# Two mixture-of-experts stages: the last experts' answers as rows, paired half-block experts, additions placed ahead, and a stored result split by tiles

## The chip, the cores and the metric

The kernel is one launch on 1 core of a Trainium2 chip. The time is the device time of that core in microseconds (us). Before the change the median of three runs is 1690.21 us (1686.34 to 1697.15).

## The reference, cut to what matters

A two-layer perceiver works on x (512 tokens of 512 numbers, float32) with a context of 8192 tokens. Each layer adds cross attention, self attention and a mixture-of-experts feed-forward stage (FFN) to x. The change lies in the two FFN stages and in the store of the final x.

```python
x = x + _L0_xattn_ref(_layernorm(x), ctx_1024, ...)
x = x + _L0_attn_ref(_layernorm(x), ...)
x = x + _L0_ffn_ref(_layernorm(x), router, W1, W2)     # 8 experts, 512 -> 2048 -> 512, silu
x = x + _L1_xattn_ref(_layernorm(x), ctx_1024, ...)
x = x + _L1_attn_ref(_layernorm(x), ...)
x = x + _L1_ffn_ref(_layernorm(x), Wg, W1, W2)         # 8 experts, 512 -> 1024 -> 512, relu squared
...
    top_v, top_i = jax.lax.top_k(logits, 2)            # each token goes to 2 of the 8 experts
    ...
    for e in range(E):
        h = act(xf @ W1[e])
        out = out + gates[:, e:e + 1] * (h @ W2[e])
```

## The kernel before, in words

**Experts by rank.** In `ffn` the router's two choices for each token are counted, and the experts are ordered by how many tokens they have (`by_rank`, L1584). The expert of rank r has room for `caps[r]` tokens (`CAPS0` for the first layer, `CAPS1` for the second, L38 and L39); all rooms lie one after another along one axis, rank r beginning at `starts[r]`. A flag says whether some expert has more tokens than room; then `rest` (L1942) works off what is left under `tc.If(flag > 0)` (L1937). In the runs here the flag is 0, and every engine jumps over that block.

**Pieces.** An expert's hidden width is cut into n pieces of 512 (n = 4 in the first layer, 2 in the second). Each piece needs 1 MB of W1 and 1 MB of W2, loaded by `weights` (L1715) from SyncE's queue (SP) into four buffers each; piece i+4's load waits until piece i's matmuls have left the buffer. `hidden(i)` (L1816) computes the hidden layer of piece i transposed: 16 matmuls (L1826) with a 128x128 block of W1 as the stationary operand and the expert's k tokens as the columns that stream; ScalarE and VectorE apply the activation (`silu` L2020, `relu_squared` L2025). `back(i)` (L1833) does the same with W2 (L1842) and gathers an expert's answer in one PSUM tile `y`, transposed; after the last piece ScalarE and VectorE copy it to `answers` (L1851, L1853). The loop at L1884 runs hidden(i) and then back(i-1), so that TensorE has a piece to work on while the activation of the next is made. A float32 matmul is two records in the profile (two passes), a transpose one.

**Tokens in, answers out.** Tokens of rank 0 are gathered by matmul (`gather`), the others by indirect DMA in blocks of 128 rows (`transposed`, L1798), each transposed on TensorE (L1811) and copied by ScalarE (L1812). Answers go the opposite way in blocks of 128 rows: `store` (L1863) transposes a block with `rows_of` (TensorE L1858, ScalarE L1860 into one of two `yb` buffers) and GpSimd's queue (POOL) writes it to DRAM (L1867). When all are stored, eight indirect DMAs on POOL fetch for each tile of 128 tokens its first and second answer (`got`, L1912), and eight VectorE operations add them, times their gates, to x (L1920).

**The last experts.** The experts from `by_dma` on don't pass through DRAM: 112 rows of room in both layers (one expert of 112 in the first, two of 64 and 48 in the second; `split` is where they begin, `tail` their size). Their answers are turned into rows (`yb`, L1921) and multiplied by a gated one-hot matrix `gb` (L1917) in the final matmul (L1925). Another matmul adds x itself through the identity (L1924). In the first layer `x_from` (L216) takes statistics of the sum (L219, VectorE) and copies it to x (L220, ScalarE); in the second layer the sums are only copied to x (L1931).

**Order.** Each engine executes its list of instructions in order. The order across pieces comes from a scheduler that sees this code, so a wait keeps back whatever stands behind it on its engine. After the flag's block the final x is stored by one 1 MB DMA (`store_x`, L2056, issued by SP); then all engines load one more number (L2071) and jump over a second block (L2075) that a larger count would need.

Of the kernel before, what the change touches and what calls it, by code (L numbers as in the profile page):

```python
# [10 lines left out]
F32 = mybir.dt.float32  # L11
# [5 lines left out]
ALU = mybir.AluOpType  # L17
# [3 lines left out]
P = 128  # L21
# [16 lines left out]
CAPS0 = (132, 160, 152, 148, 140, 124, 116, 112)  # L38
CAPS1 = (112, 256, 224, 192, 160, 96, 64, 48)  # L39
BAND = 64  # L40
# [17 lines left out]
def tile_perceiver(  # L58
# [1649 lines left out]
    def ffn(wp, pool, w1, w2, ff, layer, act, softmax_first, caps, order):  # L1708
# [20 lines left out]
        with ExitStack() as st:  # L1729
# [23 lines left out]
            def get(i):  # L1753
                if i not in pieces and i < E * n:
                    pieces[i] = weights(experts[i // n], i % n)
                return pieces.get(i)

# [5 lines left out]
            accs = {}  # L1763

            by_dma = E - 1
            while total - starts[by_dma - 1] <= P:
                by_dma -= 1
            split = starts[by_dma]
            tail = total - split

            def one_hot(to, r, gated):
# [26 lines left out]
            def transposed(b):  # L1798
# [15 lines left out]
                return go  # L1814

            def hidden(i):  # L1816
                r, c = divmod(i, n)
                k = caps[r]
# [13 lines left out]

            def back(i, hT):  # L1833
                r, c = divmod(i, n)
                k = caps[r]
# [19 lines left out]
            def rows_of(src, lo, m, name, bufs=2):  # L1855
                ps = psum.tile([P, S], F32, name="stp", tag="m")
                for c in range(NC):
                    nc.tensor.transpose(ps[0:m, c * P : (c + 1) * P], src[:, c, lo : lo + m], ident)  # L1858
                to = inner.tile([P, S], F32, name=name, tag=name, bufs=bufs)
                nc.scalar.copy(to[0:m, :], ps[0:m, :])  # L1860
                return to
# [21 lines left out]
            last, done, blk = None, 0, 0  # L1883
            for i in range(E * n):  # L1884
                hT = hidden(i)
                for j in range(1, 4):
                    get(i + j)
                if last is not None:
# [8 lines left out]
                if i % n == n - 2 and r + 1 < E:  # L1897
                    while waiting and waiting[0][0] * P < starts[r + 1] + caps[r + 1]:
                        waiting.pop(0)[1]()
                        fetch()  # L1900
# [4 lines left out]
                if i == n * by_dma + 1:  # L1905
# [11 lines left out]
                    gb = rows_of(gated, 0, tail, "gb", 1)  # L1917
            back(E * n - 1, last)
            for got, g, t in late:
                nc.vector.scalar_tensor_tensor(x[:, t, :], got, g, x[:, t, :], ALU.mult, ALU.add)  # L1920
            yb = rows_of(answers, split, tail, "yb")  # L1921
            for t in range(NT):
                ps = psum.tile([P, D], F32, name="xps", tag="h", bufs=4)
                nc.tensor.matmul(ps, lhsT=ident, rhs=x[:, t, :], start=True, stop=False)  # L1924
                nc.tensor.matmul(  # L1925
                    ps, lhsT=gb[0:tail, t * P : (t + 1) * P], rhs=yb[0:tail, :], start=False, stop=True
                )
                if layer == 0:
                    x_from(t, ps)
                else:  # L1930
                    (nc.scalar.copy if t % 2 else nc.vector.tensor_copy)(x[:, t, :], ps)  # L1931

# [4 lines left out]
        with tc.If(flag > 0):  # L1937
            rest(wp, pool, weights, irow, place, gate, xn, n, act, caps)
            for t, st in stats.items():
                nc.vector.bn_stats(st, x[:, t, :])  # L1940
# [114 lines left out]

    def store_x():  # L2056
        nc.sync.dma_start(out=out.rearrange("b (t p) d -> p (b t) d", p=P), in_=x)

# [10 lines left out]
    rest_of_layer1()  # L2069
    store_x()  # L2070
    n = nc.values_load(  # L2071
# [3 lines left out]
    with tc.If(n > SLOTS):  # L2075
# [16 lines left out]
        rest_of_layer1()  # L2092
        store_x()

# [108 lines left out]
```

## Time and profile before

| | us |
|---|---|
| median of three runs | 1690.21 (1686.34 to 1697.15) |
| the profiled execution | 1685.11 |
| its span, first to last instruction | 1683.3 |
| busy in the span: TensorE (PE) / its weight loads (PEld) | 1551.2 / 925.3 |
| busy: VectorE (DVE) / ScalarE (ACT) / GpSimd (POOL) | 767.9 / 601.5 / 449.7 |
| mean granted TensorE clock | 0.946 of full |
| last piece's matmuls of the second layer end | 1658.74 |
| last copy of the sum into x ends | 1672.61 |
| the store of x is issued, and its time to landing | 1673.61, 5.5 |

The profiled execution lies 1.8 us above its span and 5.1 us below the median. In timeline rows the columns are start, duration, engine, line, operation and tiles, count, and in brackets the idle time of that engine before it and what ended the idle time. Rows whose engine ends in q are of an engine's sequencer. "Chain" rows give start, duration and what the end of the program depended on.

### The profile page before, as it was taken

How to read it: one execution, taken by the hardware profiler on the slowest of the kernel's cores; microseconds unless marked ns; L12 is line 12 of the kernel's file. 1: busy time of each engine (PE TensorE's matmuls, PEld its weight loads, DVE VectorE, ACT ScalarE, POOL GpSimd, SP SyncE). 2: the span in 40 equal slices, each digit the busy share in tenths (PEclk: the TensorE clock that was granted, in tenths of full speed). 3: DMA queues.
4: the chain of work that ended last, by engine and by line, in shares of the span. 5: the costliest groups of instructions: out<-in, count | busy, mean ns of one | idle time of the engine just before them, and what ended most of it. 6: DMA issues, size and time to landing. Idle time of an engine off the chain costs nothing. (4 is left out here: it accounts for less than half of the span.)

```text
span 1683.3 us, 25532 instructions
## 1 busy us (share of the span) xinstructions
PE 1551.2 (92%) x10565; PEld 925.3 (55%) x10565; DVE 767.9 (46%) x1373; ACT 601.5 (36%) x1132; POOL 449.7 (27%) x345
## 2 busy tenths in 40 slices
PE   5899899999999986999999899999999999879996
PEld 2344333333244446999998456433433245469995
DVE  5366677775525553111112133667775518631101
ACT  2366365556632241111111311165557522301110
POOL 6000077777110011000002100078786110010001
PEclk9999899999999897999999999989999999779996
DMA  7155100000120005877785400000000220075562
GB/s 251 48 183 164 50 1 1 1 2 1 46 86 1 1 2 217 318 255 266 272 307 165 132 26 19 26 1 1 1 1 1 106 57 2 26 277 205 194 227 85
DMA packets 83936, 169.42 MB, mean 101 GB/s; under 512 B 5107, under 2 KB 20499, under 8 KB 82385
## 3 DMA queue, kind: packets, MB, share of 16 engines
q1 hardware_dynamic: 77200, 147.87, 26.0%
q0 software_dynamic: 6016, 17.55, 3.0%
q10 hardware_dynamic: 576, 2.10, 0.4%
q8 instruction: 89, 1.46, 0.4%
q14 instruction: 55, 0.44, 0.1%
HBM read 156.82 MB, written 9.63 MB: 99 GB/s over the span
## 5 line engine op out<-in xcount | busy, mean ns | idle before, releaser
L911 ACT ACTIVATE pT<-sc,kbias 128x512 f32<-128x512 f32 x480 | 298.3, 694 | 184.7 <-PE sc L667 142.6
L786 PE MATMUL sc<-qTf,kTf 32*128 32x512 f32 x1264 | 299.2, 657 | 2.0 <-DVE mx L799 1.1
L799 DVE SCALAR_TENSOR_TENSOR mx<-scm,kbias,mx 128x512 f32<-128x512 f32 x312 | 219.3, 745 | 72.4 <-PE scm L786 69.9
L786 PE MATMUL scm<-qTf,kTf 32*128 32x512 f32 x656 | 224.4, 670 | 10.2 <-DVE mx L799 10.2
L1842 PE MATMUL y<-hT,w 128*128 128x112 f32 (+13 forms) x1536 | 212.0, 298 | 1.1 <-DVE hT L2023 1.1
L1842 PEld LDWEIGHTS y<-hT,w 128*128 128x128 f32 x1536 | 205.4, 198 | 2.9 <-DVE hT L2023 1.2
L1826 PE MATMUL hps<-tokens,w 128*128 128x112 f32 (+13 forms) x1536 | 205.9, 293 | 0.0
L1826 PEld LDWEIGHTS hps<-tokens,w 128*128 128x128 f32 x1536 | 198.9, 192 | 1.7
L882 POOL TENSOR_TENSOR four<-four,pT 128x2048 f32<-128x2048 f32 x42 | 190.7, 4540 | 9.5 <-ACT pT L911 6.8
L786 PEld LDWEIGHTS sc<-qTf,kTf 32*128 32x128 f32 x1264 | 83.8, 187 | 121.0 <-issue 78.1
L861 PE MATMUL acc<-pT,vNf 128*32 128x256 f32 (+1 forms) x1600 | 146.5, 438 | 1.6 <-ACT o L871 1.6
L882 POOL TENSOR_TENSOR four<-pT 128x2048 f32<-128x2048 f32 x24 | 109.0, 4542 | 93.5 <-ACT pT L911 93.5
L799 DVE SCALAR_TENSOR_TENSOR mx<-sc,kbias,mx 128x512 f32<-128x512 f32 x136 | 93.2, 744 | 66.4 <-PE sc L786 66.4
L2023 DVE TENSOR_TENSOR hT<-sg,hps 128x264 f32<-128x264 f32 (+7 forms) x64 | 27.9, 437 | 191.1 <-ACT sg L2022 191.1
L861 PEld LDWEIGHTS acc<-pT,vNf 128*32 128x32 f32 x1600 | 32.1, 108 | 133.5 <-issue 127.7
L667 PE MATMUL sc<-shift,ones 3*128 3x512 bf16 (+3 forms) x544 | 95.0, 377 | 3.6 <-DVE shift L702 3.6
L1867 POOL DMA_DIRECT2D answers_d<-yb x17 | 9.4, 557 | 311.6 <-ACT yb L1860 311.6
L786 PEld LDWEIGHTS scm<-qTf,kTf 32*128 32x128 f32 x656 | 75.4, 190 | 17.8 <-DVE mx L799 17.8
L2022 ACT ACTIVATE sg<-hps 128x264 f32<-128x264 f32 (+7 forms) x64 | 25.4, 397 | 134.7 <-PE hps L1826 134.7
L2028 DVE TENSOR_TENSOR hT<-sg 128x224 f32<-128x224 f32 (+7 forms) x32 | 14.7, 459 | 107.7 <-ACT sg L2027 107.7
L1053 PE MATMUL pv<-wkvf,cslot 128*128 128x512 f32 x120 | 59.8, 641 | 3.4 <-ACT vNf L1062 3.3
L681 DVE TENSOR_REDUCE neg<-mtp 128x4 f32<-128x512 f32 x64 | 41.2, 684 | 40.2 <-PE mtp L678 40.2
(354 smaller groups left out, 1893.8 us busy)
## 6 DMA issues: line engine op xcount, KB each, us to landing
w<-in_L_ffn_W SPq DMA_DIRECT2D x96, 1024.0 KB, 7.6
mi<-in_mask SPq DMA_DIRECT2D x32, 512.0 KB, 4.3
cslot<-in_ctxT SPq DMA_DIRECT2D x30, 256.0 KB, 5.2
answers_d<-yb POOLq DMA_DIRECT2D x15, 256.0 KB, 7.1
answers_d<-zero POOLq DMA_DIRECT2D x9, 256.0 KB, 7.8
wkvf<-in_L_xattn_WkvT ACTq DMA_DIRECT2D x4, 512.0 KB, 6.6
wq<-in_L_xattn_WqT SPq DMA_DIRECT2D x2, 1024.0 KB, 8.5
wof<-in_L_xattn_WoT SPq DMA_DIRECT2D x2, 1024.0 KB, 4.7
```

The lines of the kernel that those rows point to most:

```text
L667: nc.tensor.matmul(ps, lhsT=ones16[r, :], rhs=k.shifts[g][r, 0:w], start=start, stop=stop)
L681: nc.vector.tensor_reduce(neg[:, h, :], tp.rearrange("p (t k) -> p t k", k=P), AX.X, ALU.max, negate=True)
L786: nc.tensor.matmul(ps, lhsT=kT[HD * h : HD * (h + 1), g, i * P : (i + 1) * P], rhs=qT[HD * h : HD * (h + 1), g, :], start=True, stop=stop,)
L799: nc.vector.scalar_tensor_tensor(to, ps, b, to, ALU.add, ALU.max)
L861: nc.tensor.matmul(k.sums[g][HD * h : HD * (h + 1), r], lhsT=vN[:, i, g * P + HD * h : g * P + HD * (h + 1)], rhs=pT[:, h, r], start=(i == ...
L882: engine.tensor_tensor(to, parts[g][-1], pT, ALU.add)
L911: nc.scalar.activation(pT[:, h, :], ps, AF.Exp, bias=kbias[:, i : i + 1])
L1053: last = nc.tensor.matmul(ps.rearrange("p (g n) -> p g n", g=NG), lhsT=src[:, c, s % 2, :], rhs=wkv[:, :, c, i * P : (i + 1) * P], start=( ...
L1826: nc.tensor.matmul(ps[:, j, 0:k], lhsT=w1[:, c, f * P : (f + 1) * P], rhs=tokens[:, c, starts[r] : starts[r] + k], start=(c == 0), stop=(c ...
L1842: nc.tensor.matmul(accs[0][:, d, 0:k], lhsT=w2[:, f, d * P : (d + 1) * P], rhs=hT[:, f, 0:k], start=(c == 0 and f == 0 and d % 2 == 0), st ...
L2022: nc.scalar.activation(sg, ps, AF.Sigmoid)
L2023: nc.vector.tensor_tensor(dst, sg, ps, ALU.mult)
```

## The change

The room of the last expert of the second layer grows from 48 to 64, so its last two experts fill half a block of 128 rows each; the sum of rooms becomes 1168 and takes a tenth block of 16 rows in the gather. These two experts are then worked side by side, in two units in place of four: unit c holds piece c of both. `hidden_rows` uses the tokens (128x64) as the stationary operand and streams W1 (512 columns); the first expert writes PSUM partitions 0 to 63, the second 64 to 127, matmul by matmul in turn. The activation runs once over 128x512, `transposed_rows` turns the result for the second product, and `back_rows` again streams W2 past 64 stationary columns for each expert, so that `y` holds rows. In the first layer the last expert (112 tokens) keeps `hidden` and only uses `back_rows`, with one expert. No answers of the last experts are copied to `answers` or transposed. The eight additions of `got` to x stand ahead of the last `back` in the code. In the second layer the matmul through the identity is gone; VectorE adds the product to x, and each tile of x is stored by its own 256 KB DMA, in front of the flag's block (and again inside it).

```diff
--- before.py
+++ after.py
@@ -36,7 +36,7 @@
 
 RANKS = (4, 0, 1, 2, 3, 5, 6, 7)
 CAPS0 = (132, 160, 152, 148, 140, 124, 116, 112)
-CAPS1 = (112, 256, 224, 192, 160, 96, 64, 48)
+CAPS1 = (112, 256, 224, 192, 160, 96, 64, 64)
 BAND = 64
 PAD = BAND // 2
 NW = S // BAND
@@ -1751,9 +1751,9 @@
             pieces = {}
 
             def get(i):
-                if i not in pieces and i < E * n:
+                if i not in pieces:
                     pieces[i] = weights(experts[i // n], i % n)
-                return pieces.get(i)
+                return pieces[i]
 
             for i in range(3):
                 get(i)
@@ -1761,12 +1761,19 @@
             tokens = inner.tile([P, NC, total], F32, name="tokens", tag="tokens", bufs=1)
             answers = inner.tile([P, NC, total], F32, name="answers", tag="answers", bufs=1)
             accs = {}
+
 
             by_dma = E - 1
             while total - starts[by_dma - 1] <= P:
                 by_dma -= 1
             split = starts[by_dma]
             tail = total - split
+            pair = E - by_dma == 2
+            assert pair and caps[by_dma:] == (P // 2,) * 2 or by_dma == E - 1
+            units = n * (by_dma + 1)
+            order_of = [[i] for i in range(n * by_dma)]
+            order_of += [[(r * n) + c for r in range(by_dma, E)] for c in range(n)]
+            inline = [i for u in order_of for i in u]
 
             def one_hot(to, r, gated):
                 for t in range(NT):
@@ -1813,7 +1820,55 @@
 
                 return go
 
+            def hidden_rows(i):
+
+                ws = [get(j)[0] for j in order_of[i]]
+                ps = psum.tile([P, S], F32, name="hrow", tag="h", bufs=4)
+                for c in range(NC):
+                    for j, w in enumerate(ws):
+                        lo = split + j * P // 2
+                        nc.tensor.matmul(
+                            ps[j * P // 2 : (j + 1) * P // 2, :], lhsT=tokens[:, c, lo : lo + P // 2], rhs=w[:, c, :],
+                            start=(c == 0), stop=(c == NC - 1),
+                        )
+                rows = inner.tile([P, S], F32, name="hN", tag="hN", bufs=2)
+                act(inner, rows, ps)
+
+                def transposed_rows():
+                    tp = psum.tile([P, NC, P], F32, name="htp", tag="m")
+                    for f in range(NC):
+                        nc.tensor.transpose(tp[:, f, :], rows[:, f * P : (f + 1) * P], ident)
+                    hT = inner.tile([P, NC, W], F32, name="hT", tag="hT", bufs=2)
+                    nc.scalar.copy(hT[:, :, 0:P], tp)
+                    return hT
+
+                return transposed_rows
+
+            def back_rows(i, hT):
+
+                c = i - n * by_dma
+                if pair:
+                    hT = hT()
+                if c == 0:
+                    accs[0] = pacc.tile([P, NC, W], F32, name="y", tag="y")
+                y = accs[0].rearrange("p d k -> p (d k)")[:, 0:D]
+                ws = [get(j)[1] for j in order_of[i]]
+                m = tail // len(ws)
+                for f in range(NC):
+                    for j, w in enumerate(ws):
+                        nc.tensor.matmul(
+                            y[j * m : (j + 1) * m, :], lhsT=hT[:, f, j * m : (j + 1) * m], rhs=w[:, f, :],
+                            start=(c == 0 and f == 0), stop=(c == n - 1 and f == NC - 1),
+                        )
+                if c < n - 1:
+                    return None
+                to = inner.tile([P, S], F32, name="yb", tag="yb", bufs=2)
+                nc.scalar.copy(to[0:tail, :], y[0:tail, :])
+                return to
+
             def hidden(i):
+                if pair and i >= n * by_dma:
+                    return hidden_rows(i)
                 r, c = divmod(i, n)
                 k = caps[r]
                 w1, _ = get(i)
@@ -1831,6 +1886,8 @@
                 return hT
 
             def back(i, hT):
+                if i >= n * by_dma:
+                    return back_rows(i, hT)
                 r, c = divmod(i, n)
                 k = caps[r]
                 _, w2 = get(i)
@@ -1881,10 +1938,10 @@
             for _ in range(3):
                 fetch()
             last, done, blk = None, 0, 0
-            for i in range(E * n):
+            for i in range(units):
                 hT = hidden(i)
-                for j in range(1, 4):
-                    get(i + j)
+                for j in inline[: inline.index(order_of[i][0]) + 4]:
+                    get(j)
                 if last is not None:
                     back(i - 1, last)
                     if i % n == 0:
@@ -1895,7 +1952,8 @@
                 last = hT
                 r = i // n
                 if i % n == n - 2 and r + 1 < E:
-                    while waiting and waiting[0][0] * P < starts[r + 1] + caps[r + 1]:
+                    end = total if r + 1 == by_dma else starts[r + 1] + caps[r + 1]
+                    while waiting and waiting[0][0] * P < end:
                         waiting.pop(0)[1]()
                         fetch()
                 if i == 1:
@@ -1915,20 +1973,21 @@
                             )
                             late.append((got, gates[:, j, t : t + 1], t))
                     gb = rows_of(gated, 0, tail, "gb", 1)
-            back(E * n - 1, last)
             for got, g, t in late:
                 nc.vector.scalar_tensor_tensor(x[:, t, :], got, g, x[:, t, :], ALU.mult, ALU.add)
-            yb = rows_of(answers, split, tail, "yb")
+            yb = back(units - 1, last)
             for t in range(NT):
                 ps = psum.tile([P, D], F32, name="xps", tag="h", bufs=4)
-                nc.tensor.matmul(ps, lhsT=ident, rhs=x[:, t, :], start=True, stop=False)
+                if layer == 0:
+                    nc.tensor.matmul(ps, lhsT=ident, rhs=x[:, t, :], start=True, stop=False)
                 nc.tensor.matmul(
-                    ps, lhsT=gb[0:tail, t * P : (t + 1) * P], rhs=yb[0:tail, :], start=False, stop=True
+                    ps, lhsT=gb[0:tail, t * P : (t + 1) * P], rhs=yb[0:tail, :], start=(layer > 0), stop=True
                 )
                 if layer == 0:
                     x_from(t, ps)
                 else:
-                    (nc.scalar.copy if t % 2 else nc.vector.tensor_copy)(x[:, t, :], ps)
+                    nc.vector.tensor_tensor(x[:, t, :], x[:, t, :], ps, ALU.add)
+                    store_x(t)
 
 
         flag = nc.values_load(
@@ -1936,6 +1995,9 @@
         )
         with tc.If(flag > 0):
             rest(wp, pool, weights, irow, place, gate, xn, n, act, caps)
+            if layer > 0:
+                for t in range(NT):
+                    store_x(t)
             for t, st in stats.items():
                 nc.vector.bn_stats(st, x[:, t, :])
 
@@ -2053,8 +2115,8 @@
         for t in range(NT):
             nc.sync.dma_start(out=x[:, t, :], in_=a["x"][0, t * P : (t + 1) * P, :])
 
-    def store_x():
-        nc.sync.dma_start(out=out.rearrange("b (t p) d -> p (b t) d", p=P), in_=x)
+    def store_x(t):
+        nc.sync.dma_start(out=out[0, t * P : (t + 1) * P, :], in_=x[:, t, :])
 
     c8 = const.tile([P, NKT], U8, name="c8")
     nc.sync.dma_start(out=c8, in_=a["key_mask"])
@@ -2067,7 +2129,6 @@
     nc.vector.tensor_tensor(worst, irow0[:, SLOTS : SLOTS + 1], irow1[:, SLOTS : SLOTS + 1], ALU.max)
     cross_slots1(irow1, kbias1)
     rest_of_layer1()
-    store_x()
     n = nc.values_load(
         worst, min_val=0, max_val=2 * NKT,
         skip_runtime_bounds_check_because="a count of at most NKT, or that and NKT",
@@ -2090,7 +2151,6 @@
                 osb.append(o)
             cross_attention1()
         rest_of_layer1()
-        store_x()
 
 
 # ---- launch: one core; the host lays the inputs out ----
```

## The prediction, made blind

> **What bounds the kernel now.** I read the page first, for busy shares and clock.
>
> ```profile
> PE 1551.2 (92%) x10565; PEld 925.3 (55%) x10565; DVE 767.9 (46%) x1373; ACT 601.5 (36%) x1132; POOL 449.7 (27%) x345
> PE   5899899999999986999999899999999999879996
> PEclk9999899999999897999999999989999999779996
> ```
>
> TensorE bounds nearly every slice. The change touches only the ends of the two FFN stages: about 895 to 935 us, and 1618 us to the end. So next come the chain of waits in order of time at the end, and busy time and clock of two stretches (the column before the last two is the clock).
>
> ```profile
> 1642.30 3.56 PE hps L1826 x32
> 1645.86 12.89 PE y L1842 x64
> ...
> 1659.05 0.04 DVE answers L1853
> ...
> 1662.67 2.08 PE xps L1924 x2
> ...
> 1672.02 0.59 ACT x L1931
> ```
>
> ```profile
> 1642.00:1644.00 2.00, 2.00 (x20) 2.00 (x20) 0.29 (x1) 0.35 (x2) 0.00 (x0) 1.00 0.00 0
> 1648.00:1650.00 2.00, 2.00 (x11) 2.00 (x11) 0.00 (x0) 0.00 (x0) 1.70 (x2) 0.50 0.27 49
> ```
>
> The last expert (48 tokens) takes 12.89 us for 64 records because the clock is halved; then VectorE's additions begin, and TensorE waits for them until 1662.67. Beside this runs another chain, seen in the timeline of POOL, VectorE and SP:
>
> ```profile
> 1645.11 0.54 POOL L1867 DMA_DIRECT2D answers_d<-yb  x1 [4.65 <-ACT yb L1860]
> 1647.75 1.02 POOL L1912 DMA_INDIRECT got<-answers_d,rows_of  x1 [2.11 <-DMA answers_d<-yb]
> 1656.61 0.94 POOL L1912 DMA_INDIRECT got<-answers_d,rows_of  x1 [0.30 <-DMA got<-answers_d,rows_of]
> 1659.22 5.38 DVE L1920 SCALAR_TENSOR_TENSOR x<-got,gates,x 128x512 f32<-128x512 f32 x8
> 1673.61 0.40 SPq L2057 DMA_DIRECT2D out_x<-x  x1
> ```
>
> The gathers start 2.64 us after the last store is issued, are issued over 8.9 us and land 3.7 us later (1660.3). Without TensorE's slow stretch they are what is late next.
>
> **The second layer, step by step, in the times of before.** The built order of the changed kernel gives the sequence.
>
> *Pair units.* A 512-column record costs 0.43 us here (two records of L1925 in 0.86). A pair layer is 8 matmuls, 16 records: 6.9 us one after another, 3.43 us if the two halves of 64 columns run at once. No 64-column pair is in the trace; the nearest row has four groups of 32 columns:
>
> ```profile
> 1164.81 3.48 PE den L891 x32
> ```
>
> 32 records of 512 columns in 3.48 us, where 13.8 would be one after another: 3.9 of 4. The Trainium skill speaks against full overlap: "TensorE: Matmul & The Clock Gate", Part 3, has 2.38 for three column tiles, 0.79 of ideal; two would then give 1.6, 4.3 us a layer, and three such layers ahead of the stores would cost 2.6 us more. I take the row, 3.43; the bounds are 3.43 and 6.9.
>
> *To the last store.* Before, hidden(12) began at 1618.33. Added: four transposes for the tenth block, 0.44 (0.11 each). Then hidden pair 3.43, back(11) unchanged 3.57: 1625.8. Then one matmul of the next hidden pair (0.86), eight transposes (0.9), about 0.5 waiting for ScalarE's copy of the turned rows (0.59), and the rest of two pair layers (6.9): 1635.0. Now, in the last unit, four blocks of answers are stored: transposes 0.44, copy 0.59, first store at 1636.3. There are two yb buffers, so the third copy waits for that store to land (4.0 us for the stores at 1634, 2.7 for those at 1639; I take 4.0): 1640.3. The 16-row copy follows the second store's landing, and its store goes at 1641.5, against 1645.11 before. Weights don't hold this up: the last W2 load waits for back(11), so it is issued at 1626.0 (before 1625.65), lands 5.9 us later and is needed after 1641.
>
> *Gathers and additions.* First gather 1641.5 + 2.64 = 1644.1; last issued 8.9 later, landed 3.7 later: 1656.7. In VectorE's new order the eighth addition (0.75) and then three of the new additions of the product (0.68 each, as L749's 681 ns) follow: 1659.5. Before, x was complete at 1672.6: **13.1 us gained**. One new addition stands between additions five and six: if TensorE were late it would hold back six to eight.
>
> *TensorE beside this.* Transposes of the gate block and of the last hidden rows wait for PSUM buffers until about 1641.6. So TensorE stands nearly idle from 1637.5. The same page, Part 1, says that the clock falls after an idle window of about 3.4 us. The row above shows more: it fell while TensorE was never idle (2.00 of 2.00), on 48-column matmuls. By the row alone 512-column work keeps full clock: last pair layer 3.43, four products 3.4. By the rule both double. I take the rule: 1642.4 + 6.9, copy 0.6, products 6.9: 1656.8, just under the 1657.4 at which the last three additions begin. The removed identity matmuls (4 x 0.86), answer copies and transposes lay on the old chain and are in the 13.1.
>
> *The end.* Before, 10.7 us lay between the last copy and the end. SP's waits:
>
> ```profile
> SPq L2057 <- DVEq L1937: 41.8, 1, 41.8
> SPq L2075 <- SPq L2075: 5.6, 1, 5.6
> SPq L1937 <- SPq L1937: 5.0, 1, 5.0
> ```
>
> SP took its jump at L1937 (5.0) long before, hidden in the 41.8 us wait; the store waited for VectorE to jump, 1.0 us after x was ready. Now the stores stand ahead of that jump and wait for VectorE, so behind the last of them SP makes both jumps in the open. After x: 0.1 to the issue, 0.8 for it and a load, jump one, 0.5, jump two, 0.6, and 2.6 to the end as before. The first I take as 4.5 (VectorE's took 2.9 with DMA quiet, SP's 5.4 from branch to next instruction), the second as 3.6 (TensorE's; SP's 5.7 ran beside the 1 MB store): 12.7, **2.0 lost** (bounds 0.3 gained, 5.0 lost). The store in tiles (256 KB, four issues of 0.4 on SP) gains nothing itself: its landing is covered by the jumps.
>
> **The first layer.** One expert of 112 uses all columns, so its second layer is 8 records x 0.43 = 3.43 in place of 3.57 a piece; no more. The gain is at its end:
>
> ```profile
> 921.10 0.75 DVE L1920 SCALAR_TENSOR_TENSOR x<-got,gates,x 128x512 f32<-128x512 f32 x1 [3.65 <-DMA got<-answers_d,rows_of]
> 921.77 0.39 DVE L1853 COPY answers<-y 128x224 f32<-128x224 f32 x1
> 922.68 0.59 ACT L1860 COPY yb<-stp 112x512 f32<-112x512 f32 x1 [3.04 <-PE stp L1858]
> 928.78 0.70 DVE L219 BATCH_NORM_STATS2 ln_s<-xps 128x6 f32<-128x512 f32 x1 [1.02 <-PE xps L1925]
> ```
>
> The answer's copy stands behind the eighth addition, and everything behind the copy. Now y ends about 917.6 (its last half of hT still waits behind additions until 915.8), rows are copied by 918.3, and the sums of tiles 0 to 2 (1.72 each) are done by 923.4. Tile 3 waits for the addition (921.85) and TensorE: 925.1, statistics to 925.9, against 929.5: **3.6 gained** (2 to 5; the eighth gather's landing stays).
>
> **At nothing.** The tenth block's gather (0.95 on POOL) and one more DMA that clears DRAM (0.54) lie under TensorE's work, as do the larger gate columns on VectorE; uncovered they cost 1.5.
>
> **The sum.** 13.1 - 2.0 + 3.6 = 14.7 us: span 1683.3 to 1668.6, its execution 1685.1 to 1670.4. The median of the runs lies 5.1 above that execution: 1690.2 - 14.7 = **1675.5**.
>
> **Rivals.**
> - *The halves do not overlap, at full clock.* For it: no 64-column pair in the trace. Against: den at 3.9 of 4. Three layers on the path cost 3.43 more each, 10.3: gain 4.4, 1685.8.
> - *They do not overlap and the half-filled array lets the clock fall* (slower). For it: the 48-token expert, at 0.50 with a busy TensorE. A pair layer then costs 13.7, 10.3 more; three ahead of the stores 30.9; and the last layer, copy and products (21 us) outlast the gathers by about 5: 14.7 becomes 21 lost, 1711. It decides from a pair layer of about 8.3 us up (14.7 / 3 + 3.43).
> - *Stores and gathers are slow.* Stores beside weights landed in 7.4 to 7.8 us, and the last gather of the first layer some 3.5 later than its fellows. Two such waits take 7: gain about 7.5, 1682.5. Against: at 1636 no weights are loading.
> - *More is gained*: short jumps (2.9), stores in 2.7, first layer 5: gain about 20, 1670.
>
> **How the numbers follow.** Main case 0.62, no overlap 0.10, slow stores 0.13, more gained 0.11, slower 0.04. The range, 1667 to 1688, reaches over all but the slower case and adds the spread of the three runs; the main case's own is 1671 to 1681. A difference of 1% is about what a measurement of this kernel tells from no change; here that is 16.9 us. Faster by more: a quarter of the main case, nearly all of "more gained" and some spread, 0.36. Slower by more than 1%: 0.05. Within: 0.59.
>
> **What would show it.** Two hrow records start within some nanoseconds, and a pair layer takes about 3.4 us; last store near 1638 (1641.5 less the first layer's 3.6), gathers end the waits of the last additions; SP's two jumps follow the last store; the first layer's last statistics near 925.9 us. Wrong: a pair layer near 7 us, VectorE waiting for xps rather than got, a clock of 0.5 between 1615 and 1632.

## The result and the profile after

The changed kernel takes 1673.74 us (median of 4 runs, 1671.15 to 1676.57) against 1692.31 us for the kernel before (4 runs, 1686.34 to 1697.15): ratio 0.9889, 95% interval 0.9854 to 0.9924. The forecast was 1675.5 us.

The profiled execution of the change took 1676.57 us (span 1674.8), the slowest of its runs; that of before took 1685.11, a little less than the fastest of its four timed runs. So the two spans differ by only 8.5 us, less than the medians. To compare them I tie both to an event just ahead of the change that the change doesn't touch: the first record of the sixth expert's piece in the second layer (96 columns, `hps<-tokens,w`). It lies at 1602.86 us before and at 1605.11 after: 2.25 us of drift, which falls away. From there to the end are 80.44 us before and 69.69 after: **10.75 us gained at the end**. For the first layer the event is the first 112-column record of the last expert (884.33 and 890.02): from it to the end of the last statistics are 45.15 us before and 41.76 after, **3.4 gained there**. The two fit each other: 5.69 us of drift less 3.4 is 2.3, about the drift that is left at the second event. Together 14.15 are gained; the prediction's sum was 14.7. Set against the 1690.2 us of before that gives 1676.1; the median of the runs is 2.3 better, within their spread. The two medians differ by 18.6 us, 4.4 more than the two ends account for; with an interval of some 6 us to each side the runs don't tell this from 14.15.

The page of the kernel after: busy shares, and the slices of TensorE and its clock.

```profile
PE 1535.3 (92%) x10273; PEld 885.4 (53%) x10273; DVE 767.3 (46%) x1366; ACT 599.6 (36%) x1124; POOL 451.2 (27%) x347
PE   5899999999999987999999799999999999779994
PEclk9999899999998987999999999979999999969997
```

TensorE has 16 us less work, and its share is as before. What counts is the end, in the timeline of all engines (start, duration, engine, line, operation).

```profile
1621.22 3.65 PE L1830 MATMUL hrow<-w,tokens 128*64 128x512 f32 x16
1634.37 3.60 PE L1859 MATMUL y<-w,hT 128*64 128x512 f32 x14
1643.62 0.54 POOL L1924 DMA_DIRECT2D answers_d<-yb  x1 [0.27 <-ACT yb L1917]
1645.21 5.42 PE L1859 MATMUL y<-w,hT 128*64 128x512 f32 x16 [0.68 <-ACT hT L1842]
1646.30 1.03 POOL L1970 DMA_INDIRECT got<-answers_d,rows_of  x1 [2.13 <-DMA answers_d<-yb]
1651.39 3.70 PE L1983 MATMUL xps<-yb,gb 128*128 128x512 f32 x8 [0.76 <-ACT yb L1866]
1655.87 1.20 POOL L1970 DMA_INDIRECT got<-answers_d,rows_of  x1 [0.30 <-issue]
1661.70 0.75 DVE L1977 SCALAR_TENSOR_TENSOR x<-got,gates,x 128x512 f32<-128x512 f32 x1 [2.32 <-DMA got<-answers_d,rows_of]
1662.37 1.88 DVE L1989 TENSOR_TENSOR x<-x,xps 128x512 f32<-128x512 f32 x3
```

The first row is a pair layer: 16 records of 512 columns in 3.65 us. Two records start within 0.01 us of each other and the next two 0.43 to 0.48 later, so the halves run at once. TensorE's last product is done at 1655.1; the eighth addition starts at 1661.70, held by the gather and by nothing of TensorE. The chain of waits that ended last says the same:

```profile
1655.87 5.81 DMA got<-answers_d,rows_of
...
1661.70 0.04 DVE x L1977
...
1663.56 0.68 DVE x L1989
```

Before, this chain ran through TensorE's 12.89 us of products and its sums; now it runs through the gathers. The clock by stretches of the kernel after (the column before the last two):

```profile
1640.00:1642.00 2.00, 0.37 (x4) 0.08 (x1) 0.00 (x0) 0.07 (x1) 0.59 (x2) 1.00 0.62 229
...
1646.00:1648.00 2.00, 2.00 (x8) 0.64 (x6) 0.00 (x0) 0.00 (x0) 1.40 (x2) 0.50 0.04 8
...
1650.00:1652.00 2.00, 1.24 (x6) 0.37 (x3) 1.18 (x2) 0.59 (x1) 1.54 (x2) 1.00 0.66 211
...
1664.00:1666.00 2.00, 0.00 (x0) 0.00 (x0) 0.24 (x1) 0.00 (x0) 0.00 (x0) 0.50 1.00 370
```

TensorE is nearly idle from 1640 to 1642, runs at half clock in the first half of the last pair layer, and is back at full clock for the four products. The last row is for SP: the last stores of x fill the DMA engines then (share 1.00). The waits of SP's queue in the last 25 us (in all, times, longest):

```profile
SPq L2119 <- DVE x L1989: 33.9, 4, 28.8
SPq L2136 <- SPq L2136: 2.6, 1, 2.6
SPq L1996 <- SPq L1996: 2.6, 1, 2.6
```

Behind the stores (L2119, the last issued by 1664.6) SP takes both jumps in the open, 2.6 us each, where they had cost 5.0 (hidden) and 5.6 before. The first runs from 1665.3 to 1667.9, so beside the last 0.3 MB of the stores, the second with hardly any transfer beside it. The first layer:

```profile
924.12 0.59 ACT L1866 COPY yb<-y 112x512 f32<-112x512 f32 x1 [7.52 <-PE y L1859]
...
927.14 0.75 DVE L1977 SCALAR_TENSOR_TENSOR x<-got,gates,x 128x512 f32<-128x512 f32 x1 [1.15 <-DMA got<-answers_d,rows_of]
...
931.08 0.70 DVE L219 BATCH_NORM_STATS2 ln_s<-xps 128x6 f32<-128x512 f32 x1 [1.02 <-PE xps L1983]
```

The answers are copied rows by 924.71, 2.4 us ahead of the eighth addition; behind that stand only TensorE's sums of the last tiles (1.72 a tile) and their statistics.

### The profile page after: what moved, and what is told of

The parts are those of the page before. It is cut to its first block, busy times and chain, and to the rows that moved or that the text cites. A ratio compares the mean times of both kernels' runs of the same rounds, so it can differ in the third digit from the quotient of the medians.

```text
span 1674.8 us, 24933 instructions
## 1 busy us (share of the span) xinstructions
PE 1535.3 (92%) x10273; PEld 885.4 (53%) x10273; DVE 767.3 (46%) x1366; ACT 599.6 (36%) x1124; POOL 451.2 (27%) x347
## 5 line engine op out<-in xcount | busy, mean ns | idle before, releaser
L1881 PE MATMUL hps<-tokens,w 128*128 128x160 f32 (+11 forms) x1408 | 191.1, 294 | 0.0
L1881 PEld LDWEIGHTS hps<-tokens,w 128*128 128x128 f32 x1408 | 184.2, 192 | 2.2 <-issue 0.5
L1899 PE MATMUL y<-hT,w 128*128 128x160 f32 (+11 forms) x1280 | 176.2, 296 | 0.0
L1899 PEld LDWEIGHTS y<-hT,w 128*128 128x128 f32 x1280 | 170.3, 193 | 2.5 <-issue 0.8
L1053 PE MATMUL pk<-wkvf,cslot 128*128 128x512 f32 x120 | 54.8, 599 | 4.4 <-DVE kb L1092 4.4
```

What stands on the lines that cost most here:

```text
L1053: last = nc.tensor.matmul(ps.rearrange("p (g n) -> p g n", g=NG), lhsT=src[:, c, s % 2, :], rhs=wkv[:, :, c, i * P : (i + 1) * P], start=( ...
L1881: nc.tensor.matmul(ps[:, j, 0:k], lhsT=w1[:, c, f * P : (f + 1) * P], rhs=tokens[:, c, starts[r] : starts[r] + k], start=(c == 0), stop=(c ...
L1899: nc.tensor.matmul(accs[0][:, d, 0:k], lhsT=w2[:, f, d * P : (d + 1) * P], rhs=hT[:, f, 0:k], start=(c == 0 and f == 0 and d % 2 == 0), st ...
```

## The experiments

The table has, for each kernel, the ratio to the kernel before with its interval (0.15 to 0.36% to each side, 2.5 to 6 us), and from its one profiled execution four times in us counted from the first 96-column record: the first gather's issue, the end of the additions of gathered rows, x complete, and the end.

| kernel | ratio | first gather | additions end | x complete | end |
|---|---|---|---|---|---|
| before | 1 | 44.89 | 61.74 | 69.75 | 80.44 |
| after | 0.9889 (0.9854 to 0.9924) | 41.19 | 57.34 | 59.14 | 69.69 |
| e1_no_pair | 0.9928 (0.9901 to 0.9955) | 44.89 | 62.82 | 65.51 | 75.84 |
| e2_one_store_behind | 0.9887 (0.9862 to 0.9912) | 41.20 | 57.14 | 58.93 | 69.32 |
| e6_one_store_ahead | 0.9920 (0.9891 to 0.9949) | 41.17 | 57.49 | 59.29 | 71.68 |
| e5_halves_in_turn | 0.9934 (0.9914 to 0.9954) | 45.64 | 62.15 | 63.95 | 75.09 |
| e4_room_64 | 1.0001 (0.9983 to 1.0019) | 43.74 | 61.26 | 69.50 | 80.22 |
| e4_again | one execution, 1683.1 us | 43.75 | 56.97 | 65.50 | 75.85 |
| e10_no_pair_room_64 | 0.9931 (0.9903 to 0.9958) | 43.74 | 58.06 | 59.85 | 71.65 |
| e10_again | 0.9952 (0.9937 to 0.9967) | 43.74 | 62.12 | 63.92 | 74.65 |
| e7_four_answer_tiles | 0.9899 (0.9863 to 0.9935) | 39.40 | 54.43 | 56.22 | 66.61 |
| e8_held_jumps | 0.9911 (0.9879 to 0.9943) | 41.21 | 55.62 | 57.42 | 70.52 |
| e9_together | 0.9897 (0.9864 to 0.9931) | 39.40 | 54.47 | 55.27 | 66.68 |
| e11_by_tile_four_stores | 0.9892 (0.9856 to 0.9927) | 39.40 | 55.55 | 56.35 | 66.78 |

**Theory**: the pairs and the missing transposes bring the stores and the gathers forward, x is complete when the gathers are, and what is lost behind it is SP's jumps. **Rivals**: the pairing is worth little and the rest does it; or the halved clock of the 48-column expert was the loss, and a room of 64 cures that alone.

**Without pairs.** The second layer's last two experts as before (rooms 64 and 48, one after another), all else of the change kept.

```diff
-CAPS1 = (112, 256, 224, 192, 160, 96, 64, 64)
+CAPS1 = (112, 256, 224, 192, 160, 96, 64, 48)
-            pair = E - by_dma == 2
+            pair = False
```

(and the loops over units that follow from it)

> Second layer's last two experts as in the kernel before (rooms 64 and 48, answers copied and transposed); the first layer's rows, the code order of the additions and the store by tiles stay. Counted from the start of the 96-token hidden layer of piece 10 to the end of the span: before 80.4 us, changed kernel 69.7 us. My theory (the pair lets stores, gathers and additions start 3.6 us earlier and frees them from TensorE's halved clock): x complete only behind the last y, about 76 us to the end, so only some 4 us of the second layer's 10.8 are kept, and with the first layer's 5 the ratio to before is near 0.994. Rival (the gain of the second layer is the missing identity matmul and the early store in tiles): it keeps about 70 us and a ratio near 0.989.

Measured: 75.84 to the end, 6.15 more than with pairs, 4.6 less than before. That is as expected. So the pairing and its room of 64 carry more than half of the end's gain, and the rest of the change (no identity products, stores by tile) what is left. The table says where: from the end of the additions to x complete are 8.0 us before and 2.7 here, which I read as the part of the missing identity product; from there to the end it hardly changes (10.7 and 10.3). What the pairs add is an earlier end of the additions (62.8 to 57.3). No run leaves the identity product alone in place.

**Halves one after another.** The order of matmuls in a pair layer: all of one half, then all of the other.

```diff
-            for c in range(NC):
-                for j, w in enumerate(ws):
+            for j, w in enumerate(ws):
+                for c in range(NC):
```

(and likewise for the products in `back_rows`)

> The changed kernel with each pair layer's four matmuls of one expert first and then the four of the other, so that neighbours use the same columns. My theory: no overlap, a pair layer takes 6.9 us in place of 3.5, three of them lie ahead of the stores: last store 10 us later, 80 us from piece 10 to the end, ratio to before near 0.997. Rival (the halved array lets the clock fall): pair layers of 13.7 us and 95 us or more. Rival (the engine overlaps them whatever the order): 69.7 us.

Measured: 75.09, between no overlap (80) and full overlap (69.7), so none of the three expectations came. A pair layer takes 5.42 us:

```profile
1623.42 5.42 PE L1830 MATMUL hrow<-w,tokens 128*64 128x512 f32 x16
```

In the trace of its records the second half's first starts 1.77 us after the first half's first, beside the latter's fifth: four records alone, four pairs, four alone, twelve steps of 0.43 and the rest of the last one. The second half's first record starts ahead of the first half's sixth, seventh and eighth, which stand before it in the order. So a record may overtake those queued ahead of it on the other half, here by about four; the order of the change, alternating, overlaps them all. This shows that the 3.4 us of a pair layer come from the overlap, and not from rows in place of columns.

**The stores of x.** I believed first that the last gather lands late (5.81 us after its issue, 3.6 before) because the first tiles' stores run beside it. One store of 1 MB in their place, behind the branch as before (e2), or ahead of it (e6):

```diff
-                    store_x(t)
...
     rest_of_layer1()
+    store_x()
```

> The changed kernel with one 1 MB store of x behind the flag's block, as before. My theory (the first tile's store, issued at 1657.9 beside the last gather, delays its landing from 3.7 to 5.8 us, and the early store gains nothing at the end because the jumps then lie in the open): last gather lands in 3.7 us, x complete 2 us earlier, end 10.7 us after that as before, 67.7 us from piece 10 to the end. Rival (store by tiles saves the landing of a large store): 72 us or more.

> The changed kernel with one 1 MB store ahead of the flag's block. My theory: last gather lands in 3.7 us as nothing is stored beside it, x complete 2 us earlier; SP then jumps twice beside a 1 MB transfer, where a jump took 5 to 6 us before in place of 2.6: 12 to 15 us from x complete to the end, 69 to 72 us from piece 10. Rival (tiles themselves matter): last gather still lands late, 72 us or more.

Measured: additions end at 57.14 and 57.49, as with the four stores (57.34). That theory falls: the stores don't delay the gather. Nor do they gain: behind the branch the single store ends 0.4 earlier in the profile, and the ratio is the same. Ahead of the branch it costs 2.0 in the profile: from x complete to the end 12.39 us in place of 10.55. There SP's first jump lies beside the whole transfer and takes 4.7, the second takes 2.7:

```profile
SPq L1997 <- SPq L1997: 4.7, 1, 4.7
SPq L2136 <- SPq L2136: 2.7, 1, 2.7
```

**The additions' place.** Moving the loop of additions behind the last `back` again, as before, leaves the order of instructions on every engine as it is, because the scheduler sets that order. So this edit does nothing by itself in this kernel.

**The room of 64.** One number in the kernel before.

```diff
-CAPS1 = (112, 256, 224, 192, 160, 96, 64, 48)
+CAPS1 = (112, 256, 224, 192, 160, 96, 64, 64)
```

> The kernel before with one number changed: the last expert of the second layer gets a room of 64 tokens in place of 48, so its matmuls are 64 columns wide; no halves side by side, all else as before. It asks what halved the clock in the last expert. If the narrow shape did (48 columns at 0.50), 64 columns stay at full clock: the 64 records of its second layer take about 7.1 us (by the 3.56 us of 32 records ahead of them) in place of 12.89, x is ready some 5 us earlier until the gathers hold it, and the time is about 1686. If the clock falls at this point of the kernel whatever the width, they take 13 to 14 us and the time is 1690 to 1691.

> The kernel before with the room of 64, profiled once more: does ScalarE's copy of the last answers again begin 4 to 5 us behind the end of the last record of the second layer (then the records' ends are not the end of the work there, or the signal of it is held), or within 0.2 us of it, as with the room of 48 (then the first profile was an accident, and the end comes some 4 to 5 us earlier, about 75 us after the last 96-token piece begins in place of 80.2)?

The two profiles, each with the second layer's products and ScalarE's copy behind them (first e4_room_64, with its clock between them at 1648, then e4_again):

```profile
1644.97 7.31 PE L1842 MATMUL y<-hT,w 128*128 128x64 f32 x64
1656.85 0.27 ACT L1851 COPY answers<-y 128x128 f32<-128x128 f32 x1 [11.40 <-remote]
```

```profile
1648.00:1650.00 2.00, 2.00 (x21) 2.00 (x20) 0.00 (x0) 0.00 (x0) 1.70 (x2) 1.00 0.68 168
```

```profile
1648.84 7.31 PE L1842 MATMUL y<-hT,w 128*128 128x64 f32 x64
1656.19 0.27 ACT L1851 COPY answers<-y 128x128 f32<-128x128 f32 x1 [6.87 <-PE y L1842]
```

At 64 columns the clock stays at 1.00 and the 64 records take 7.31 us: the width of 48 halved it, not the place. But the time of the kernel before doesn't move (1.0001), against the 1686 us expected. In the first profile the copy starts 4.57 us after the last record's end. "Remote" means that the profile finds no instruction that ended just then; in the trace the semaphore that TensorE's products raise moves at 1656.83. In the second profile the copy starts at once, which shows that the products can be done in 7.31 us, and the end is 4.4 us earlier. Ends of matmuls are modelled in a profile, so the first profile alone doesn't tell a late signal from products that took longer than their records say.

**No pairs, room of 64.** All of the change but the pairing (e1 with the room of e4).

> The run without side-by-side halves, with the last expert's room raised from 48 to 64 tokens: all of the change except the pairing. The profile of the room of 64 in the kernel before showed 64 records of the last second layer at full clock, 7.31 us for 12.89, but ScalarE's copy behind them began 4.57 us after the last of them ended and the time did not move. Theory A (the halved clock was most of what pairing saved; the late copy there was that profile's accident): the products are done some 5 us earlier than without the room, the gathers are last, the end comes 70 to 71 us after the last 96-token piece begins (75.84 with the room of 48, 69.69 with pairs), about 1673. Theory B (records that end early do not release ScalarE early; the pairing is worth its 6 us whatever the clock): 75 to 76, about 1678.

> The changed kernel without pairing and with the room of 64, a second time. Its first profile had the end 71.65 us after the last 96-token piece begins, 4.2 less than without the room (75.84) and 2.0 more than with pairs (69.69); its timed ratio, 0.9931, was that of the run without the room (0.9928). If the room's full clock is worth what the profile shows, this profile has 71 to 72 again and the ratio is about 0.990. If the signal that the products are done is late in many executions, as in the first profile of the room of 64 in the kernel before, the ratio is 0.993 again, and this profile may show 75 to 76.

Measured: 71.65 and 74.65 to the end, the second with a copy that again starts 4.3 us after the records; ratios 0.9931 and 0.9952. By the profiles alone the pairing is worth 2.0 us over a full-clock single expert when the signal comes at once, and 5.0 when it doesn't. By the times the pairs win, narrowly: their interval ends at 0.9924, that of the second run begins at 0.9937, while that of the first (0.9903 to 0.9958) overlaps theirs. Neither run is told from e1 either, whose room is 48. What delays the signal in two of four profiles isn't shown; in none of the kernels with pairs did I see it.

**Four buffers for the turned rows.** The third and fourth copy of the last unit waited for a store to land (2.22 us in the profile after).

```diff
-                to = inner.tile([P, S], F32, name="yb", tag="yb", bufs=2)
+                to = inner.tile([P, S], F32, name="yb", tag="yb", bufs=4)
-            def rows_of(src, lo, m, name, bufs=2):
+            def rows_of(src, lo, m, name, bufs=4):
```

> The changed kernel with four buffers for the turned answer rows in place of two, so that the third and fourth block's copies wait for no store. My account of the last unit (the copies wait for the first store's landing, and the gathers for the last store): the last store is issued some 2.5 to 3 us earlier, TensorE's wait for the last turned hidden rows is shorter by as much, the first gather starts at about 38.5 us after the last 96-token piece begins (41.2 now), and the end comes 2.5 to 3 us earlier, 67 us after that point (69.7 now): about 1671, ratio 0.987. Rival (the end hangs on TensorE's last products or on DMA transfers that come at their own time): the first gather moves but the end doesn't, 69 to 70, 1673.5.

```profile
1634.84 1.07 POOL L1924 DMA_DIRECT2D answers_d<-yb  x2 [0.30 <-ACT yb L1917]
1638.49 1.02 POOL L1970 DMA_INDIRECT got<-answers_d,rows_of  x1 [2.58 <-DMA answers_d<-yb]
```

The last stores go without a wait, the first gather 1.8 us earlier, and the profile ends 66.61 after its event, 3.1 less than after and as expected. The rest of the 3.1 is the last gather's: it lands 3.7 us after its issue here, not 5.8. The ratio, 0.9899, doesn't show the gain: 3 us are 0.2%, and the interval is 0.36% to each side.

**Jumps held back.** TensorE and ScalarE come to their first jump over the code of the branch 16 and 23 us earlier than before (1651.8 and 1651.4, where they had jumped at 1665.2 and 1672.4, drift counted), and to the second at 1656.9 and 1655.9, while the last gathers run. During the jumps the trace has DMA packets of the kind "instruction" (8 to 16 KB each) among those of the gathers. A matmul on the finished x, and a ScalarE copy of it, ahead of the branch, hold the jumps.

```diff
+            if layer > 0:
+                ps = psum.tile([P, D], F32, name="held", tag="h", bufs=4)
+                nc.tensor.matmul(ps[:, 0:P], lhsT=ident, rhs=x[:, NT - 1, 0:P], start=True, stop=True)
+                to = inner.tile([P, S], F32, name="yb", tag="yb", bufs=2)
+                nc.scalar.copy(to[:, 0:P], ps[:, 0:P])
```

> The changed kernel with one small matmul that reads the last tile of the finished x, and a ScalarE copy of its result, put ahead of the branch at the end of the last feed-forward layer: TensorE and ScalarE can't take their jumps (and fetch the code behind them) while the gathers run, only after x is complete. Theory A (the instruction fetches of these early jumps slow the last gathers, 5.8 us from the last one's issue to its landing against 3.7 before): the gathers are issued 0.95 us each again, and the last one lands in 3.5 to 4 us; the additions of gathered rows end near 55 us after the last 96-token piece begins (57.3 now). Behind it three engines now jump at once, so the end itself can be 1 to 4 us longer than the 10.55 now. Rival B (the last gather is late for a reason of its own, the additions ahead of it or the DMA engines): additions still end at 57.3, and the time is 1674 or more.

```profile
1654.44 0.95 POOL L1970 DMA_INDIRECT got<-answers_d,rows_of  x1 [0.30 <-DMA got<-answers_d,rows_of]
...
1658.15 0.75 DVE L1977 SCALAR_TENSOR_TENSOR x<-got,gates,x 128x512 f32<-128x512 f32 x1 [0.81 <-DMA got<-answers_d,rows_of]
```

The last gather is landed 3.71 us after its issue, not 5.81, and the additions end 1.7 earlier: theory A holds for the landing. e10's first profile agrees: there ScalarE (1655.7) and TensorE (1656.4) jump just as its last gather is issued (1655.97), and that one alone takes 4.67, the others 3.4 to 3.8. So do the other profiles: the last gather takes 5.7 to 5.9 us in the four where both engines begin their second jump about when it is issued or later (after, e2, e5, e6), and 3.5 to 3.7 in the four where neither jumps beside it (before, e1, e4_again, e10_again). In e7 and e11, where TensorE's jump had begun 2.7 and 2.4 us ahead of the issue, it takes 3.7 and 4.9. The spacing of the issues didn't come back (9.95 us from first to last), so that part of theory A falls. And the jumps cost more elsewhere: from x complete to the end are 13.10 us now, 2.55 more.

**Together**: four buffers, gathers by tile of x, one store behind the branch (e9), or the four stores (e11).

```diff
-                    for j in range(2):
-                        for t in range(NT):
+                    for t in range(NT):
+                        for j in range(2):
```

> The changed kernel with three edits: four buffers for the turned answer rows, gathers ordered by tile of x (both of a tile next to each other) so that only one tile's additions stand behind the last gather, and one store of x behind the branch in place of the four in two places. If each is worth what it should: 2.5 to 3 from the buffers, 1.5 to 2 from two of the three additions behind the last gather, 0.3 from the store: the end comes 64.5 to 65.5 us after the last 96-token piece begins (69.7 now), some 1668.5 to 1669.5. If the end is held by TensorE's products: 67 or more, 1671.

> The kernel with four buffers for the turned answer rows, with the gathers of a tile of x next to each other, and the four stores of x ahead of the branch as in the changed kernel. The run with one store behind the branch had x complete at 55.3 us after the last 96-token piece begins, against 56.2 with the gathers in their old order, but 11.4 us from there to the end against 10.4. If the order of the gathers is worth this 0.9 to 1 and the four stores keep the short end: 65.5 to 65.8 us to the end (66.6 with the buffers alone), about 1669.5. If the short end was chance: 66.6 or more.

Both end 66.7 to 66.8 after the event, one to two us later than expected: the gathers' order is worth nothing measurable over the four buffers alone. In e9 x is complete 0.95 earlier than in e7, and from there to the end it takes 11.41 in place of 10.39; in e11 x isn't complete any earlier. In e2, with the same single store as e9, that stretch took 10.39, so a microsecond between single profiles is not to be explained. By the ratios none of e2, e7, e9 and e11 is told from the change itself.

## Why the prediction was right, and where its terms were off

In the times of before (after, less 2.25 us):

| step | forecast | measured |
|---|---|---|
| a pair layer | 3.43 | 3.65 with the last record's end; step 0.43 |
| first of the last four stores issued | 1636.3 | 1637.3 |
| the third copy begins | 1640.3 | 1639.7 |
| last store issued | 1641.5 | 1641.4 |
| first gather issued | 1644.1 | 1644.05 |
| last gather issued | 1653.0 | 1653.6 |
| last gather landed | 1656.7 | 1659.4 |
| x complete | 1659.5 | 1662.0 |
| from x complete to the end | 12.7 | 10.55 |
| gain in the second layer | 11.1 | 10.75 |
| gain in the first layer | 3.6 | 3.4 |

- **The pairs overlap, and this is what moves the stores.** The row of four groups of 32 columns was the right neighbour: 16 records in 3.65 us are 1.9 of 2. The rule that I set against it (the Trainium skill, "TensorE: Matmul & The Clock Gate", Part 3: 2.38 for three column tiles, which is 0.79 of ideal) would make it 4.3, an estimate from that figure; the measurement decides for the row. The rivals without overlap are out; e5 shows what a part of the overlap is worth.
- **The last store and the first gather came within 0.1 us, by luck.** TensorE was behind by small slips, 0.5 us at the end of back(11), and the first of the last four stores went 1.0 late. The wait for the third buffer made up for it: it is there, as forecast, but the store landed 2.3 us after its issue and not 4.0. The prediction had a 4.0 and a 2.7 in its rows and took the longer. The rows of the kernel after (in its own times):

```profile
1639.52 1.07 POOL L1924 DMA_DIRECT2D answers_d<-yb  x2 [7.37 <-ACT yb L1917]
1641.93 0.59 ACT L1917 COPY yb<-stp 128x512 f32<-128x512 f32 x1 [2.22 <-DMA answers_d<-yb]
```

- **Mis-sized: the gathers.** "Last issued 8.9 later, landed 3.7 later" carried two durations over from a stretch in which VectorE was waiting and TensorE and ScalarE had work. Now they took 9.57 and 5.81, 2.7 us more. The 2.1 of the landing are the freed engines' jumps beside it (e8: 3.71 without them). The prediction had asked what follows TensorE's end only up to x, and not that the engine then jumps. The wider issues stood in the kernel before, in its first layer, where VectorE's additions do run beside the gathers:

```profile
904.04 1.02 POOL L1912 DMA_INDIRECT got<-answers_d,rows_of  x1 [2.80 <-DMA answers_d<-yb]
907.45 0.75 DVE L1920 SCALAR_TENSOR_TENSOR x<-got,gates,x 128x512 f32<-128x512 f32 x1 [2.98 <-DMA got<-answers_d,rows_of]
913.69 1.22 POOL L1912 DMA_INDIRECT got<-answers_d,rows_of  x1 [0.30 <-issue]
```

From the first issue to the last are 9.65 us there, with no pair and before TensorE or ScalarE jumps. In the first layer of all fourteen profiles the span is 9.5 to 9.8. In the second it is 9.5 to 10.1 in seven of the eight kernels with pairs (9.0 in e9), and 8.8 to 8.9 in the six without, whose additions begin behind the last issue or beside the last two at most. So the wider spacing goes with the additions, and neither pairs nor these jumps are needed for it. It is not shown that they cause it: some issues beside an addition stay at the usual 1.25 us, and holding the additions back wasn't tried.

- **Mis-sized: SP's jumps at the end.** "2.0 lost" was a gain of 0.1. The first was taken as 4.5 and the second as 3.6, between short and long rows; both took 2.6, the first although the last 0.3 MB of the stores moved beside it. e6, whose first jump lies beside the whole 1 MB, needs 1.8 more from x to the end.
- The two errors, 2.5 us later and 2.1 us earlier, nearly cancel, which is luck: the total is right to 0.6 us while two of its terms were off by more.
- **The clock.** The fall that the same page's Part 1 states for an idle window came (1.00 up to 1642, 0.50 in the stretch from 1646 to 1648), though TensorE was not wholly idle ahead of it: sixteen transposes ran between 1637.9 and 1640.4, and then 1.6 us were empty. But the clock was back at 1648.8, after 6.8 us and within the pair layer. So this layer took 5.42 us and not 6.9, and the four products 3.70 and not 6.9. All of it lay under the gathers, as forecast. And the other view holds too: in the kernel before, 48-column work halved the clock on a TensorE that was always busy; e4 shows 1.00 there at 64 columns.
- **The reading of the bound.** The prediction began with the 12.89 us of half clock. e4 shows that curing these alone doesn't move the median. Of its two profiles one ends 4.6 us earlier than before, the other only 0.2, with the late copy; how often the copy is late isn't known. The gathers were the next limit, as the second chain said: in e4_again the eighth addition waits for the last of them.
- **The first layer** came as worked out: the gain is the answers' copy and transposes taken from behind the eighth addition. This is read from the trace; no run takes the first layer's edit alone. The place of the additions in the text had no part in it.

## What to carry to other kernels

Two series of matmuls of half the array's width overlapped in full only where their instructions alternated (3.65 us a layer, 5.42 one half after the other); write that order out. Look for a term's size in a row taken under the conditions it will meet: the wider spacing of the gathers stood in the first layer. Where a chain gets shorter, ask what the engines that are free earlier do next: here their jumps lay beside the last gathers and took back 2 of 13 us. And tie two traces together at an event just ahead of the change before comparing ends: here 2.25 us at the end and 5.7 ahead of the first layer's end were drift.

## What the runs showed of the hardware that was not expected

- In e5, the first record of one half started beside the fifth of the other, ahead of three that stand before it in the order: four pairs of records overlapped out of eight.
- 48 columns and 64 columns took the same 0.11 us a record at full clock (3.56 us for 32; 7.31 for 64), but the clock was halved 4.4 us after the last expert's 48-column records began, and was not with 64.
- A jump of SP at the end took 2.5 to 2.8 us where at most 0.3 MB of x's stores moved beside it, and 4.7 to 5.7 where the whole 1 MB did (before, both e4, e2, e6, e9). In e8, where several engines jumped at once, its two took 3.3 and 4.3.
- In two of four profiles with a single expert of 64 columns, the semaphore of TensorE's last products came 4.3 and 4.6 us after the end of their last record. The cause stays open.
